# Moving small constants, R's sums and the stores of two output planes in a conditioned residual convolution kernel

## The chip, the cores and the metric

The kernel runs on one core of a Trainium2 chip. The metric is device time in microseconds: the median over several runs, and beside it one execution that was profiled. Engines are named as in the profile: PE is TensorE's matmuls, PEld its weight loads, DVE VectorE, ACT ScalarE, POOL GpSimd, SP SyncE, which issues most DMAs.

## What is computed

128 samples of 64 channels and 1024 positions go through four modulated 1-D convolutions with 3 taps; the input is added to the result. Each sample has its own weights, scaled by a style vector and normalised per output channel.

```python
def _layer(x, style, w, b, mw, mb, typ):
    s = style @ mw.T + mb
    weight = SCALE * w * s[:, None, :, None]
    demod = lax.rsqrt(jnp.sum(weight * weight, axis=(2, 3)) + EPS)
    weight = weight * demod[:, :, None, None]
    if typ == 'same':
        out = jax.vmap(_conv_same)(x, weight) + b[None, :, None]
    elif typ == 'upsample':
        out = jax.vmap(_conv_up)(x, weight.transpose(0, 2, 1, 3)) + b[None, :, None]
        out = _blur(out, 2.0 * blur_k, (1, 1))
    elif typ == 'downsample':
        xb = _blur(x, blur_k, (2, 2))
        out = jax.vmap(_conv_down)(xb, weight) + b[None, :, None]
    return out
...
for i, typ in enumerate(('same', 'upsample', 'same', 'downsample')):
    out = _layer(out, style, weights[i], biases[i], mod_w[i], mod_b[i], typ)
x = x + out
```

## The kernel before

There is no nonlinearity between the layers, so the kernel multiplies the four layers' weights of each sample into one 9-tap filter per pair of channels and convolves once. A few output columns at either end, and the biases, are computed apart. Everything is fp32.

The work goes in 32 groups of 4 samples, numbered q. One pass of the loop (`turn_of`, L1491, here called turn q) works on several groups at once, n = q + 1, c = q + 2 and s = q + 4: it convolves group q to its end and group n in part, and builds the filter of c and, one step further back, of s. The order of instructions on each engine is the order of the code; each engine works its own list through from the top, and waits only for what an instruction needs.

The filter of a group is made in a chain. Stage 1 (`stage1_a`, `stage1_b`, L434 and L448) gives S in the PSUM banks psS; stage 2 (`stage2`, L545) gives R in psR, which ScalarE copies to SBUF (L570). `r_sums` (L615) adds neighbouring slots of R, on GpSimd in a steady turn and on VectorE in turn 4. Stage 3 (`stage3_b`, `stage3_a`, L622 and L647) multiplies R and these sums into the taps Wf, in the banks psA and psW. psS, psR and psW share one pair of PSUM banks, so each has to wait until the last one is read. `combine_a` and `combine_b` (L713, L721) then form three combinations of the taps, h1 to h3, on VectorE; the convolution (`conv0` to `conv4`, L809) works on five combinations of the three input planes with them and with the taps.

An input group lies in one of two buffers X as three planes (every third position). Two of its combinations, T12, are made on GpSimd (`in1`, `in2`), another, T3, in most turns by ScalarE (`in3_negated`, L757) and two accumulating loads that GpSimd issues (`in3_added`, L761); those turns are the set ADDED: 4 to 9, 11 to 13, 16, 17 and 20 to 27. `load` (L141) puts six loads into SyncE's list in each turn, one for each plane and half. `outputs` (L1387) writes one output plane of both halves on ScalarE into a buffer o (two of these) and puts two stores into SyncE's list; planes 2, 1 and 0 follow each other at the end of a turn. So SyncE's list holds six loads and then six stores in each turn.

Turn 4 is the entry, the first pass of this loop (`entry`), and turns 0 to 3 (`early_turn`, L1393) have another order. Beside the turns stand small tables: EXTRA, TABLES, SIDE and LATE (L1316 to L1369) name what is done once, in which turn and where. `small` (L1295) is a small matmul for the constant of one layer into the high columns of the bank Y, `clear_high` (L1304) the memset ahead of it, `small_rest` (L1308) VectorE's use of it. In turns 4, 5 and 6 the matmul stands behind the last conv of the turn, and the rest at the very end of the turn. `tap_differences` (L476) makes differences of blur weights for stage 2, which are first needed in turn 6.

Of the kernel before, what the change touches and what calls it, by code (L numbers as in the profile page):

```python
# [55 lines left out]
K = 3  # L56
# [7 lines left out]
def kernel(  # L64
# [12 lines left out]
    NQ = B // 4  # L77
# [59 lines left out]
    NX = 2  # L137
# [3 lines left out]
    def load(q, planes=slice(0, 3)):  # L141

        if q < NQ:
            at = slice(planes.start * PL, planes.stop * PL)
            for c in range(2):
                nc.sync.dma_start(Xs[q % NX][:, c, at], x[2 * q + c, :, at])
# [117 lines left out]
    def var_newton(bs, ls=slice(0, NL)):  # L264

        newton(var[:, ls, bs], dm[:, ls, bs], nw[:, ls, bs])
# [22 lines left out]
    def table_A(bs, d):  # L289
        table(nc_v, tA, bs, slice(0, 4, 3), slice(1, 3), sc[:, 3, bs], d)  # L290
# [185 lines left out]
    def tap_differences():  # L476

        d = Ed[:, :4].rearrange("c (a b) o -> c a b o", a=2)
        for b in range(2):
            nc_g.tensor_sub(d[:, :, b], E[:, 4 * b : 4 * b + 5 : 4], E[:, 2:7:4])  # L480
        nc_g.tensor_sub(Ed[:, 4:], En[:, 1:4:2], En[:, 2:3].to_broadcast([P, 2, C]))
# [63 lines left out]
    def stage2(q, pool=None, engs=(nc_a, nc_a), between=None):  # L545
        st = chain[q]
        shared = q in shared_ps
        ps = stage2_rest(q) if shared else unit(pool or ps_w, f"psR{q}")
        for n, e in enumerate(() if shared else (-2, -1, 0, 1, 2, 3, 4, 5, 6)):
            if e % 2 == 0:  # L550
                a, lo, m, w = slice(2, 7, 2), e // 2 + 1, 3, E[:, e + 2]
            else:
                a, lo, m = slice(3, 6, 2), (e + 3) // 2, 2
                w = E[:, e + 2] if q in plain else En[:, (e + 1) // 2]
            for r, rows in enumerate(HALF):
                for c, cols in enumerate(HALF):
# [12 lines left out]
        for r in range(2):  # L569
            scaled_copy(engs[r], flat(t[:, r, :7]), ps[r][:, C : 8 * C], tC[:, q, r : r + 1])  # L570
        chain[q] = t
        return ps
# [42 lines left out]
    def r_sums(q, eng):  # L615
        t = chain[q]
        for r in (slice(0, 2),) if eng is nc_v else PAIR:
            eng.tensor_add(t[:, r, 7:10], t[:, r, 0:6:2], t[:, r, 1:7:2])  # L618
# [75 lines left out]
    def residual(q, made):  # L694

        W = Wq[q][0]
        if made:
            v = W[:, tap(1, 1)]
            nc_v.tensor_add(v, v, x3)
            return  # L700
        for r in range(2):
            v = W[:, tap(1, 1), r, :]
            nc_v.scalar_tensor_tensor(v, idn3, t3[:, q, r : r + 1], v, op0=ALU.mult, op1=ALU.add)

    def sum_of(out, x, f, y, op=ALU.add):
        nc_v.scalar_tensor_tensor(out, x, f, y, op0=ALU.mult, op1=op)  # L706
# [3 lines left out]
        merged = (*(W[:, i] for i in TAPS), *(H_[:, i] for i in range(3)))  # L710
        return [t.rearrange("c g r o -> c g (r o)") for t in merged]

    def combine_a(q, made=False):  # L713

        chain.pop(q)
        a, b, c, h1, h2, h3 = taps(q)
        sum_of(h1, c, -2.0, a)
        residual(q, made)
        sum_of(h3, h1, 1.0 / 6.0, b)

    def combine_b(q, steps=range(3)):  # L721
# [140 lines left out]
    def sum2(q, steps=(0, 1), wide=True):  # L862
        if 0 in steps:
            m3 = m3c.pop(q)
            whole = parts(q) if wide else [(s, a[:, :NB]) for s, a in enumerate(banks(q))]
            for s, a in whole:
                sum_of(Y[:, s, :NB], m3[:, s], 3.0, a)
        for s, a in parts(q) if 1 in steps else ():
            nc_v.tensor_sub(y1w[q][:, s], y1w[q][:, s], a)  # L869
# [21 lines left out]
    def store(q, s, planes=slice(0, K), queue=nc.sync):  # L891
        queue.dma_start(
            out[q, :, s, planes.start * NB : planes.stop * NB],
            os[q][:, s, planes].rearrange("c i j -> c (i j)"),
        )
# [41 lines left out]
    def vector_Da(bs):  # L937
        nc_g.tensor_mul(Da[:, bs], sc[:, 3, bs], dm[:, 2, bs])
# [8 lines left out]
    def vector_b1(bs):  # L947
        with_bias(b1s, sc[:, 2], 1, bs)

    def vector_c2(bs):  # L950
        with_bias(c2f, sc[:, 3], 2, bs)
# [352 lines left out]
    def clear_high(q):  # L1304
        _, bs = SMALL[q]
        nc_v.memset(high(bs.stop - bs.start), 0.0)

    def small_rest(q):  # L1308
        l, bs = SMALL[q]
        const_rest(l, bs, high(bs.stop - bs.start))  # L1310

    def layers(i, j):
        return REST, slice(i, j)
# [4 lines left out]
        (1, 1): lambda: (small_rest(1), tap_shares()),  # L1318
        (2, 1): lambda: (small_rest(2), var_root(REST, Y[:, 0])),
        (2, 2): lambda: (table_B(REST), vector_a1(REST)),  # L1320
        (3, 0): lambda: (var_newton(*layers(2, 3)), var_newton(*layers(0, 2))),
        (3, 1): lambda: (table_A(REST, dm[:, 2, REST]), small_rest(3)),
        (3, 2): lambda: (
            table_b(PART[1]),
            (table_0(REST), table_0_kinds()),
            vector_b1(REST),
            vector_c0(REST),
        ),
    }
# [1 line left out]

    TABLES = {
        4: lambda: table_C(REST),
        5: lambda: (vector_c2(REST), vector_Da(REST), table_3(REST), tap_differences()),
        6: zeros,
        7: lambda: table_b(REST),
        9: setup0,
# [4 lines left out]
        4: lambda: var_newton(*layers(3, 4)),  # L1342
    }

    def small_next(q):
        small_rest(q)
        clear_high(q + 1)

    LATE = {
        4: lambda: small_next(4),  # L1350
        5: lambda: small_next(5),
        6: lambda: small_rest(6),
        7: lambda: setup1(0),
        8: lambda: setup_x(0),
        9: lambda: setup_x(1),
# [20 lines left out]

    AHEAD = 3
    FIRST = AHEAD + 1
    ADDED = set(LATE)

    def sharing(q):
        return FIRST < q < NQ - 4
# [4 lines left out]
    def outputs(q, i):  # L1387
        for r in range(2):
            output(q, i, r)
            if late(q):  # L1390
                store(q, r, slice(i, i + 1))

    def early_turn(q):  # L1393
        n, c, s = q + 1, q + 2, q + 3 + (q >= AHEAD)
# [96 lines left out]
    def turn_of(q):  # L1491
        n, c, s = q + 1, q + 2, q + 4
        entry = q == FIRST
        stage2(c)
        if not entry:
            identity(n)
            if q in ADDED:
                in3_negated(c)
            elif s < NQ:
                scale3(s)  # L1500
        if entry:
            sum2(q, wide=False)
            conv4(q)
            combine_a(n)
            r_sums(c, nc_v)
            in3_negated(c)
        else:
            conv2(q)
            r_sums(c, nc_g)
            sum2(q)  # L1510
            in2(n, nc_g)
            if q in ADDED:
                in3_added(c)
        side(TABLES, q)
        if entry:
            in3_added(c)
        for i in range(3):
            load(c + 1, slice(i, i + 1))
        stage3_b(c, open_a(n), c + 1 if sharing(q) else 0)
        if q in ADDED and FIRST < q and s < NQ:  # L1520
            scale3(s)
        if entry:
            conv0(q, 0, 1)
        else:
            combine_a(n, True)
            conv4(q)
        stage3_a(c)
        combine_b(n)
        conv3(n)
        copy_m3(n)  # L1530
        conv0(q, 2 if entry else 0)
        if s < NQ:
            stage1_a(s)
        outputs(q, 2)
        in04(n)
        side(SIDE, q)
        in_g01(c)
        if entry:
            conv1(n, 0, 1)
            outputs(q, 1)  # L1540
        else:
            conv0(q, 1, 2)
        if s < NQ:
            stage1_b(s)
        if entry:
            clear_high(q)
        in_g2(c)
        if sharing(q):
            share_copy(c + 1)
        if not entry:  # L1550
            outputs(q, 1)
        outputs(q, 0)
        if q in SLOTS:
            matmuls, width, rest = SLOTS[q]
            conv1(n, 0, 1)
            slot(matmuls, width, Y_banks)
            rest()
        if s == NQ:
            slot(ends3, 3, unit(ps_w, "psE"), 3)
            rest3()  # L1560
        conv1(n, *((2,) if entry or q in SLOTS else range(K)))
        if q in SMALL:
            small(q)
        sum1(n)
        if q not in ADDED:
            in3(c)
        if sharing(q + 1):
            share_sums(s)
        if s == NQ:
            in04(c)  # L1570
        in1(c, nc_g)
        side(LATE, q)
# [153 lines left out]
```

## Time and profile before

| | |
|---|---|
| median of 3 runs | 477.87 us (477.09 to 479.24) |
| the profiled execution, whole | 477.03 us |
| its span, first to last instruction | 475.3 us |
| PE busy | 465.5 us, 98% |
| DVE, ACT, POOL busy | 399.0, 365.8, 235.0 us |
| granted PE clock, mean | 0.997 |
| moved by DMA | 77.34 MB, mean 163 GB/s |

Durations are read from the profiled execution. A matmul record counts as busy from its start to a modelled end, so a short stop inside a group of matmuls can hide in its busy time; the starts of the groups show it. In a timeline row stand the start in us, the length in us, the engine, the line, the operation, the tiles (output, then inputs) and the count, and in brackets the idle time before it and what ended it. In a row of the waits stand the total in us, how often, and the longest. In a row of a stretch (start:end) stand its length, PE's busy time and matmul records, the granted clock, the mean share of the 16 DMA engines that is busy, and GB/s. [...]

### The profile page before, as it was taken

The numbers are of one execution on the slowest core, as the hardware profiler recorded it, in microseconds if no ns is written. First come the engines' busy times: TensorE is split into PE (matmuls) and PEld (weight loads), VectorE is DVE, ScalarE is ACT, GpSimd is POOL, SyncE is SP. The second block draws the span as 40 slices with busy tenths as digits, with TensorE's granted clock in tenths as the row PEclk, the third lists the DMA queues.
The fourth block names the chain that finished last, engine by engine and source line by source line (L and its number), as shares of the span: only waits on it lengthen the run. The fifth ranks groups of instructions, "written<-read, shape, count | busy, mean of one in ns | idle before, by whom it ended". The sixth has DMA issues, their size and how long they took to land.

```text
span 475.3 us, 26462 instructions
## 1 busy us (share of the span) xinstructions
PE 465.5 (98%) x11656; PEld 346.1 (73%) x11656; DVE 399.0 (84%) x613; ACT 365.8 (77%) x871; POOL 235.0 (49%) x301
## 2 busy tenths in 40 slices
PE   8999999999999999999999999999999999999995
PEld 7977777776677786768867677757677878877652
DVE  4899999878988887888878888969888888988795
ACT  6575667679888896988877988878888889887452
POOL 3534342779755752545444557535455654543200
PEclk9999999999999999999999999999999999999998
DMA  5416264465667654677543675545777567675225
GB/s 176 148 38 224 95 198 188 151 170 141 172 180 203 197 155 147 149 182 201 182 146 126 152 182 182 172 130 123 203 188 186 179 159 196 181 177 160 97 82 192
DMA packets 55986, 77.34 MB, mean 163 GB/s; under 512 B 6272, under 2 KB 52800, under 8 KB 55872
## 3 DMA queue, kind: packets, MB, share of 16 engines
q1 hardware_dynamic: 49808, 68.32, 46.1%
q0 software_dynamic: 5472, 6.66, 9.4%
q8 instruction: 91, 1.49, 1.4%
q10 hardware_dynamic: 592, 0.69, 0.5%
q14 instruction: 23, 0.19, 0.1%
HBM read 42.01 MB, written 33.62 MB: 159 GB/s over the span
## 4 chain that ended last, share of the span: by engine, by line
PE 94%; DVE 3%; issue 1%; DMA 1%; ACT 1%; SPq 0%; ACTq 0%; DVEq 0%
PE psA L809 45%; PE Y L809 11%; PE psW L596 10%; PE psR L490 9%; PE psS L400 5%; PE psR L558 4%; PE psA L596 4%; PE psA L490 2%; PE Y L1052 2%; DMA par_s<-in_params_s 1%; PE Y L337 1%; DVE Y L706 1%; ACT o L887 0%; DVE o L889 0%; DVE H L706 0%
## 5 line engine op out<-in xcount | busy, mean ns | idle before, releaser
L809 PE MATMUL psA<-T,H 64*64 64x340 f32 x2304 | 186.7, 447 | 0.3 <-DVE y L706 0.2
L809 PEld LDWEIGHTS psA<-T,H 64*64 64x64 f32 x2304 | 90.8, 133 | 47.0 <-issue 2.6
L706 DVE SCALAR_TENSOR_TENSOR G<-X 128x684 f32<-128x684 f32 (+1 forms) x65 | 78.4, 1211 | 3.5 <-DMA X<-in_x 0.9
L809 PE MATMUL psA<-T,Wf 64*64 64x340 f32 x768 | 68.1, 446 | 0.0
L809 PE MATMUL Y<-T,Wf 64*64 64x340 f32 x768 | 62.6, 451 | 0.2
L361 ACT ACTIVATE R<-psR,tC 128x448 f32<-128x448 f32 x63 | 36.5, 630 | 31.5 <-PE psR L490 15.1
L465 POOL TENSOR_TENSOR S<-S 128x128 f32<-128x128 f32 x24 | 11.4, 477 | 95.6 <-ACT S L361 95.6
L706 DVE SCALAR_TENSOR_TENSOR Y<-m,psA 128x680 f32<-128x680 f32 (+1 forms) x40 | 29.2, 729 | 28.4 <-PE psA L809 27.4
L796 DVE TENSOR_TENSOR T<-G 128x1368 f32<-128x1368 f32 (+1 forms) x33 | 51.2, 1553 | 0.0
L782 POOL TENSOR_TENSOR T<-G 128x684 f32<-128x684 f32 x28 | 46.4, 1659 | 8.3 <-DVE G L706 8.3
L787 POOL TENSOR_TENSOR T<-G 128x684 f32<-128x684 f32 x28 | 46.6, 1664 | 0.0
L361 ACT ACTIVATE Wf<-psW,t 128x192 f32<-128x192 f32 (+1 forms) x76 | 30.0, 444 | 19.2 <-PE psW L596 18.9
L618 POOL TENSOR_TENSOR R<-R 128x192 f32<-128x192 f32 x48 | 27.8, 599 | 29.2 <-ACT R L361 29.2
L809 PEld LDWEIGHTS Y<-T,Wf 64*64 64x64 f32 x768 | 30.2, 132 | 16.4 <-DVE Y L706 1.1
L887 ACT ACTIVATE o<-psA,tb,td 128x340 f32<-128x340 f32 x63 | 36.1, 622 | 6.3 <-PE psA L809 6.3
L809 PEld LDWEIGHTS psA<-T,Wf 64*64 64x64 f32 x768 | 29.4, 133 | 14.8
L887 ACT ACTIVATE o<-Y,tb,td 128x340 f32<-128x340 f32 x63 | 36.6, 637 | 4.5 <-PE Y L809 2.6
L887 ACT ACTIVATE o<-y,tb,td 128x340 f32<-128x340 f32 x62 | 38.1, 664 | 0.6 <-DVE y L869 0.6
L706 DVE SCALAR_TENSOR_TENSOR H<-Wf 128x384 f32<-128x384 f32 x64 | 38.5, 602 | 0.0
L706 DVE SCALAR_TENSOR_TENSOR H<-H,Wf 128x384 f32<-128x384 f32 x64 | 35.9, 560 | 2.2
L361 ACT ACTIVATE S<-psS,tB 128x256 f32<-128x256 f32 (+1 forms) x63 | 26.8, 476 | 13.0 <-PE psS L400 13.0
L490 PE MATMUL psR<-S,E 64*64 64x64 f32 (+1 forms) x920 | 34.6, 239 | 0.0
(186 smaller groups left out, 1010.6 us busy)
## 6 DMA issues: line engine op xcount, KB each, us to landing
out<-o SPq DMA_DIRECT2D x167, 170.0 KB, 3.0
X<-in_x SPq DMA_DIRECT2D x150, 172.0 KB, 4.5
X<-in_x SPq DMA_DIRECT2D x14, 516.0 KB, 4.5
T<-in_x POOLq DMA_DIRECT2D x38, 171.0 KB, 5.5
out<-o SPq DMA_DIRECT2D x6, 510.0 KB, 5.2
out<-o SPq DMA_DIRECT2D x2, 340.0 KB, 2.7
Xe<-in_x_ends SPq DMA_DIRECT2D x1, 512.0 KB
out<-o ACTq DMA_DIRECT2D x3, 170.0 KB, 2.4
```

The lines of the kernel that those rows point to most:

```text
L361: nc_a.activation(dst, src, AF.Copy, scale=f)
L400: nc.tensor.matmul(ps[r][cols, at * C : (at + n) * C], weight[rows], wd[c if r == 0 else 1 - c][rows, taps], start=first, stop=last, skip_ ...
L490: nc.tensor.matmul(dst[r][cols], weight[rows], st[c if r == 0 else 1 - c][rows, slots, :], start=False, stop=last, skip_group_check=True,)
L558: nc.tensor.matmul(ps[r][cols, (lo + 1) * C : (lo + 1 + m) * C], w[rows], src[rows, a, :], start=(n == 0), stop=(n == 8), skip_group_check ...
L596: nc.tensor.matmul(dst[r][cols], weight[rows], t[rows, c, slots, :], start=first, stop=last, skip_group_check=True,)
L618: eng.tensor_add(t[:, r, 7:10], t[:, r, 0:6:2], t[:, r, 1:7:2])
L706: nc_v.scalar_tensor_tensor(out, x, f, y, op0=ALU.mult, op1=op)
L782: eng.tensor_add(t[:, :, 0, :NJ], plane(g, 2), plane(g, 1))
L787: eng.tensor_sub(t[:, :, 1, :NJ], plane(g, 2), plane(g, 1))
L796: nc_v.tensor_sub(t[:, pairs, :, :NJ], both(a, PL), both(b, 1))
L809: nc.tensor.matmul(ps[s][cols, :NB], w, Ts[q, tag][rows, c, i, g : g + NB], start=(g == 0 and m == 3), stop=(g == K - 1), skip_group_check ...
L887: nc_a.activation(dst, src, AF.Identity, bias=add, scale=d3)
```

## The change

It has five parts.

1. In turn 4 `r_sums` on VectorE goes ahead of the combination h3, by the new argument `ahead` of `combine_a`. In the same turn one group of conv 0 on TensorE moves from ahead of `stage1_a` to behind it, and one group of conv 1 from ahead of `stage1_b` to behind it.
2. `tap_differences` and two constants (`vector_c2`, `vector_b1`) move from turns 5 and 3 (its end) to the middle of turn 3, and `vector_Da` from turn 5 to turn 3.
3. The small matmuls of turns 4, 5 and 6, with what VectorE does with them, move behind stage 2 of the next turn (`small_here`).
4. The stores of planes 1 and 0 in turns 5 to 27 are held back (`to_store`) until the loads of the next turn are in SyncE's list.
5. From turn 5 on GpSimd writes one column of the input buffer behind R's sums (`gate`), a column that the next load writes too. So the loads wait for that write.

```diff
-    def combine_a(q, made=False):
+    def combine_a(q, made=False, ahead=None):
...
         residual(q, made)
+        if ahead:
+            ahead()
         sum_of(h3, h1, 1.0 / 6.0, b)
...
-        (3, 0): lambda: (var_newton(*layers(2, 3)), var_newton(*layers(0, 2))),
-        (3, 1): lambda: (table_A(REST, dm[:, 2, REST]), small_rest(3)),
+        (3, 0): lambda: (
+            (var_newton(*layers(2, 3)), var_newton(*layers(0, 2))),
+            (tap_differences(), vector_c2(REST), vector_b1(REST)),
+        ),
+        (3, 1): lambda: (table_A(REST, dm[:, 2, REST]), small_rest(3), vector_Da(REST)),
...
-        5: lambda: (vector_c2(REST), vector_Da(REST), table_3(REST), tap_differences()),
+        5: lambda: table_3(REST),
...
-    def small_next(q):
+    def small_here(q):
+        small(q)
         small_rest(q)
-        clear_high(q + 1)
+        if q + 1 in SMALL:
+            clear_high(q + 1)
...
             if late(q):
-                store(q, r, slice(i, i + 1))
+                to_store.append((q, r, slice(i, i + 1)))
+        if i == 2 or not FIRST < q < NQ - 4:
+            stores()
+
+    to_store = []
+
+    def stores():
+        while to_store:
+            store(*to_store.pop(0))
+
+    def gate(q):
+        if q < NQ:
+            nc_g.memset(Xs[q % NX][:, :, 0:1], 0.0)
...
         stage2(c)
+        if not entry and q - 1 in SMALL:
+            small_here(q - 1)
...
-            combine_a(n)
-            r_sums(c, nc_v)
+            combine_a(n, ahead=lambda: r_sums(c, nc_v))
...
             r_sums(c, nc_g)
+            gate(c + 1)
             sum2(q)
...
             load(c + 1, slice(i, i + 1))
+        stores()
         stage3_b(c, open_a(n), c + 1 if sharing(q) else 0)
...
-        conv0(q, 2 if entry else 0)
+        if not entry:
+            conv0(q, 0)
...
-            conv1(n, 0, 1)
+            conv0(q, 2)
+            conv1(n, 0)
...
-        conv1(n, *((2,) if entry or q in SLOTS else range(K)))
-        if q in SMALL:
-            small(q)
+        conv1(n, *((1, 2) if entry else (2,) if q in SLOTS else range(K)))
```

How the lists change, at three places. First GpSimd's list in turn 5 and the start of turn 6, before; R is what `r_sums` adds up, T the planes' combinations, c2f and Da the constants, wsq the weight differences, S the sums of stage 1.

```order
L618 TENSOR_TENSOR R_1882<-R_1882 128x192 x2
L787 TENSOR_TENSOR T_6_1839<-G_1798 128x2x342
L765 DMA T_7_1887<-in_x 128x342 x2
L942 TENSOR_TENSOR c2f<-sc,par_s 128x96
L938 TENSOR_TENSOR Da<-sc,dm 128x96
L287 TENSOR_TENSOR t_139<-dm,var 64x48 x2
L284 TENSOR_SCALAR td<-dm 64x48 x2
L480 TENSOR_TENSOR wsq<-E 128x2x64 x2
L481 TENSOR_TENSOR wsq<-En 128x128
L465 TENSOR_TENSOR S_2046<-S_2046 128x2x64
```

The same place after the change:

```order
L618 TENSOR_TENSOR R_1882<-R_1882 128x192 x2
L1406 MEMSET X_107 128x2
L789 TENSOR_TENSOR T_6_1842<-G_1799 128x2x342
L767 DMA T_7_1892<-in_x 128x342 x2
L287 TENSOR_TENSOR t_139<-dm,var 64x48 x2
L284 TENSOR_SCALAR td<-dm 64x48 x2
L465 TENSOR_TENSOR S_2047<-S_2047 128x2x64
```

Four of the operations between R's sums and the next turn's work on S are gone from here, and the write to X stands behind R's sums.

Second SyncE's list from turn 4 on, before; X is an input buffer (two in turn), o an output buffer.

```order
L892 DMA out<-o_1788 128x340 x6
L146 DMA X_107<-in_x 128x344 x6
L892 DMA out<-o_2049 128x340 x6
L146 DMA X_108<-in_x 128x344 x6
L892 DMA out<-o_2340 128x340 x6
```

After:

```order
L894 DMA out<-o_1789 128x340 x6
L146 DMA X_107<-in_x 128x344 x6
L894 DMA out<-o_2050 128x340 x2
L146 DMA X_108<-in_x 128x344 x6
L894 DMA out<-o_2050 128x340 x4
L894 DMA out<-o_2342 128x340 x2
```

The two stores of plane 2 stay at the end of their turn; the four of planes 1 and 0 stand behind the next turn's six loads.

Third VectorE's list in turn 4, before; H are the combinations of the taps Wf, R as above.

```order
L706 SCALAR_TENSOR_TENSOR H_1425<-Wf_1424 128x384
L703 SCALAR_TENSOR_TENSOR Wf_1424<-idn_159,t_139,Wf_1424 128x64 x2
L706 SCALAR_TENSOR_TENSOR H_1425<-H_1425,Wf_1424 128x384
L618 TENSOR_TENSOR R_1652<-R_1652 128x2x192
L706 SCALAR_TENSOR_TENSOR H_1425<-Wf_1424 128x384
```

After:

```order
L706 SCALAR_TENSOR_TENSOR H_1425<-Wf_1424 128x384
L703 SCALAR_TENSOR_TENSOR Wf_1424<-idn_159,t_139,Wf_1424 128x64 x2
L618 TENSOR_TENSOR R_1657<-R_1657 128x2x192
L706 SCALAR_TENSOR_TENSOR H_1425<-H_1425,Wf_1424 128x384
L706 SCALAR_TENSOR_TENSOR H_1425<-Wf_1424 128x384
```

R's sums have gone one step forward.

More of the change, by code (lines that the diff above doesn't have):

```diff
@@ L1325 @@
             (table_0(REST), table_0_kinds()),
-            vector_b1(REST),
             vector_c0(REST),
@@ L1343 @@
     }
-    def small_next(q):
+    def small_here(q):
+        small(q)
         small_rest(q)
-        clear_high(q + 1)
+        if q + 1 in SMALL:
+            clear_high(q + 1)
     LATE = {
-        4: lambda: small_next(4),
-        5: lambda: small_next(5),
-        6: lambda: small_rest(6),
         7: lambda: setup1(0),
@@ L1378 @@
     FIRST = AHEAD + 1
-    ADDED = set(LATE)
+    ADDED = {FIRST, FIRST + 1, FIRST + 2, *LATE}
     def sharing(q):
```

## The prediction

> **What bounds the kernel now.** I read the page first, then TensorE's waits, then the places where TensorE stops, row by row, then the DMA share of single stretches. A turn is one pass of the steady loop; turn 4 is the entry, and turns 8 and 9 serve as examples: the chain of waits has stage 2 of turn 8 at 143.63 and of turn 9 at 157.33, 13.7 us on.
>
> ```profile
> span 475.3 us, 26462 instructions
> PE 465.5 (98%) x11656; PEld 346.1 (73%) x11656; DVE 399.0 (84%) x613; ACT 365.8 (77%) x871; POOL 235.0 (49%) x301
> PE 94%; DVE 3%; issue 1%; DMA 1%; ACT 1%; SPq 0%; ACTq 0%; DVEq 0%
> ```
>
> TensorE is busy for 98% of the span and carries 94% of the chain that ended last. The change removes no matmul, so it can only win back stops. From 88 to 440 us TensorE's waits are three rows:
>
> ```profile
> PE psA L596 <- issue: 1.1, 3, 0.5
> PE Y L1300 <- DVE Y L1306: 0.6, 1, 0.6
> PE psA L596 <- DVE R L618: 0.3, 1, 0.3
> ```
>
> That is 2.0 us of idle time in 352 us. Stops inside a group that counts as busy come on top; I found those by the starts of the same groups in other turns. ```profile
> 143.63 1.94 PE psR L490 x112
> ...
> 157.33 1.94 PE psR L490 x112
> ```
>
> All together the change can win some 3 us, 0.7% of the time. A measurement of this kernel can tell about 0.5% (2.4 us) from no change, so the forecast lies close to that border.
>
> **The entry turn (4).** TensorE's rows there, then VectorE's and ScalarE's:
>
> ```profile
> 91.33 0.58 PE L596 MATMUL psA<-R,w0s 64*64 64x64 f32 x24
> 92.21 0.56 PE L596 MATMUL psA<-R,par 64*64 64x192 f32 x8 [0.29 <-DVE R L618]
> ...
> 96.75 0.80 PE L809 MATMUL psA<-T,Wf 64*64 64x340 f32 x8
> 97.33 0.52 PE L400 MATMUL psS<-wd,par 64*64 64x64 f32 x22
> ...
> 100.61 0.30 PE L1300 MATMUL Y<-c0f,wsum 64*64 64x96 f32 x2 [0.58 <-DVE Y L1306]
> ```
>
> ```profile
> 91.09 0.56 DVE L706 SCALAR_TENSOR_TENSOR H<-H,Wf 128x384 f32<-128x384 f32 x1
> 91.57 0.59 DVE L618 TENSOR_TENSOR R<-R 128x384 f32<-128x384 f32 x1
> ...
> 96.44 0.64 ACT L361 ACTIVATE Wf<-psW,t0c 128x128 f32<-128x128 f32 x2
> ```
>
> - R's sums go ahead of one step of the filter combination, so they start at 91.09 in place of 91.57: 0.48 us earlier. TensorE loses 0.53 us on them (0.88 from 91.33 to 92.21; the same 24 matmuls take 0.35 in turn 8, from 147.10 to 147.45 in the rows further down). Gain 0.48. The step that now comes second feeds the conv of plane 3, whose 24 matmuls end at 96.75; nothing waits for it earlier.
> - The 8 matmuls at 96.75 (0.57 us to 97.33) no longer stand between the conv and stage 1 of the chain. Stage 1 writes the banks that ScalarE reads until 97.08 (96.44 + 0.64), so TensorE, there at 96.75, waits for up to 0.33 us. Both engines move up together, so this stays. Cost between 0 and 0.33; I take 0.3, because the bank of the last read is also needed in the first group.
> - The small matmul no longer waits for the memset at the end of the turn; it is asked for behind the whole of the next stage 2, and the memset is done by then. Gain 0.6. The two later small matmuls move in the same way and cost the same there.
>
> Sum of the entry turn: 0.48 - 0.3 + 0.6 = 0.8 us gained.
>
> **Turn 6.** R's sums are on GpSimd here. TensorE's rows of turn 6, then of turn 8, with GpSimd's sums of turn 6 ahead and its moved work (turn 5, by groups) behind:
>
> ```profile
> 118.75 1.35 POOL L618 TENSOR_TENSOR R<-R 128x192 f32<-128x192 f32 x2
> ```
> ```profile
> 119.60 0.95 PE L596 MATMUL psA<-R,par 64*64 64x192 f32 x5
> ...
> 120.85 1.38 PE L809 MATMUL Y<-T,Wf 64*64 64x340 f32 x16
> ```
> ```profile
> 147.10 0.53 PE L596 MATMUL psA<-R,w0s 64*64 64x64 f32 x24
> 147.45 0.41 PE L490 MATMUL psA<-S,E 64*64 64x64 f32 x16
> ...
> 147.80 0.51 PE L596 MATMUL psA<-R,par 64*64 64x192 f32 x8
> ...
> 148.35 1.95 PE L809 MATMUL Y<-T,Wf 64*64 64x340 f32 x24
> ```
> ```profile
> L480 POOL TENSOR_TENSOR wsq<-E 128x128 f32<-128x128 f32 x2 | 1.5, 774 | 0.1
> L938 POOL TENSOR_TENSOR Da<-sc,dm 128x96 f32<-128x96 f32 x1 | 1.3, 1337 | 0.0
> ```
>
> From the first matmul on the sums to the next conv turn 6 takes 1.25 us (119.60 to 120.85) and turn 8 0.55 (147.80 to 148.35): 0.7 us lost, because GpSimd ends the sums at 120.10. The constants and weight differences of turn 5 (1.5 + 1.3 = 2.8 us, and two shorter operations) had pushed GpSimd back. Moved to turn 3 they fall into this idle time:
>
> ```profile
> 85.79 0.73 POOL L462 TENSOR_TENSOR S<-S 128x256 f32<-128x256 f32 x1 [10.92 <-ACT S L361]
> ```
> ```profile
> POOL S L465 <- ACT S L361: 95.6, 23, 6.4
> ```
>
> Even at twice 2.8 us it fits into 10.9, so turn 3 pays nothing; without that cover it would hold back the chain's sums. What is late next in turn 6 is ScalarE's R, as in turn 8. Gain 0.7.
>
> **The stops called issue.** In turn 9 TensorE stops inside 24 matmuls that depend on nothing new, and again in turn 19, where the group counts as busy:
>
> ```profile
> 160.80 0.51 PE L596 MATMUL psA<-R,w0s 64*64 64x64 f32 x20
> 161.65 0.27 PE L596 MATMUL psA<-R,w0s 64*64 64x64 f32 x2 [0.33 <-issue]
> ...
> 303.76 0.83 PE L596 MATMUL psA<-R,w0s 64*64 64x64 f32 x21
> ```
> ```profile
> 161.40:218.50 57.10, 56.80 (x1528) 1.00 0.61 166
> 218.50:304.05 85.55, 85.34 (x2292) 1.00 0.58 164
> 304.05:362.10 58.05, 57.70 (x1529) 1.00 0.62 166
> ```
> ```profile
> q8 instruction: 42, 0.69, 1.6%
> ```
>
> The stretches run from one such stop to the next (x is TensorE's matmuls). 1528, 2292 and 1529 are 11.9, 17.9 and 11.9 times 128. The instruction queue delivers 42 packets of 16 KB in the same 200.7 us, in which TensorE does 5349 matmuls: 127 to a packet. So the stops stand at packet borders: the next instructions have not arrived. Turn 9's costs 0.5 us (161.65 - 160.80 less 0.35 for the group), turn 19's 0.3 (0.83 against 0.53). The three idle stops sum to 1.1, with 0.33 of idle time for 0.5 lost: 1.1 x 0.5 / 0.33 = 1.7, and 0.3 for turn 19, together 2.0.
>
> [...]
>
> **Why the late stores matter for them.** DMA share of stretches, last but one number (TensorE only): the first two are the start of turn 8 and of turn 9, then two later stretches of turn 8:
>
> ```profile
> 143.90:146.40 2.50, 2.50 (x117) 1.00 0.25 76
> 157.60:160.10 2.50, 2.50 (x117) 1.00 0.64 217
> ...
> 151.60:155.20 3.60, 3.60 (x80) 1.00 0.87 188
> 155.20:157.40 2.20, 2.20 (x56) 1.00 0.38 137
> ```
>
> Turn 9 stops and turn 8 doesn't. At the start of turn 9 the DMA engines are 64% busy with the stores of planes 1 and 0, against 25%. SyncE's rows of turn 8:
>
> ```profile
> 143.81 3.09 SPq L892 DMA_DIRECT2D out<-o  x4
> 146.99 4.06 SPq L146 DMA_DIRECT2D X<-in_x  x6
> ```
>
> After the change the four stores stand behind the six loads, and the loads wait for GpSimd's write of a column behind R's sums. In turn 8 those sums lie ahead of the matmuls on them at 147.80, so the loads, which before start at 146.99, start up to 0.8 us later. The start of the turn, where stage 2 and stage 3 use up instructions fastest (117 matmuls in 2.5 us against 80 in 3.6), is then free of stores and loads. I count the 2.0 us as won, less 0.1 for a remainder: 1.9.
>
> Everything behind the gate has cover. GpSimd waits 95.6 us for stage 1 in 23 turns, 4.2 a turn; the memset that its next step waits behind fits in (no 128x2 memset is in the trace; it costs between 0 and the 0.7 of one of R's two sums, and either fits). The loads are read first in the next turn, and a turn is 13.7 us against the 4.06 that they take to issue. The stores free an output buffer that is written again two turns on.
>
> **What it costs.** The four stores do not vanish. Two plane 2 stores are what the stretch 155.2 to 157.4 holds: 0.38 x 2.2 = 0.84 us of all engines, so four take 1.7. They now follow loads and GpSimd's accumulating loads, where the share is 0.87, and fill the quieter 155.2 to 157.4 (1.36 us free). The instruction packet asked for in the second half of a turn, which now finds that quiet stretch, has to pass them. Only turns with accumulating loads are that full: 18 of them (5 to 9, 11 to 13, 16, 17, 20 to 27). Bounds: no stop, or 0.5 us (turn 9's) in all 18, 9.0. I take two to three stops, 1.2 us, the end that is nearer to turn 8, which goes through a stretch of 0.87 without a stop.
>
> Sum: 0.8 + 0.7 + 1.9 - 1.2 = 2.2 us gained. The profiled execution took 477.03 (1.7 beside its span), 0.8 below the median of 477.87; it would take 474.8. Taken off the median: **475.7**.
>
> **Rivals.**
> - The late stores cost no packet: gain 3.4, 474.5, and 473.4 if a second stop in turn 19 and delays under 0.3 us, which I left out, go too. For it: turn 8 runs through its full second half without a stop. [...]
> - The late stores stop TensorE at the turn's end instead: the packet comes behind six loads and four stores. It decides from 7 turns with a stop (3.4 / 0.5); 12 to 18 of them give 6 to 9 less 3.4, so 480.5 to 483.5. For it: 1.7 us of stores meet 1.36 us of free engines before the next turn.
> - The stops are not due to data traffic, so that part of the change does nothing: 0.8 + 0.7 gained, 476.4. Against it: the multiples of 128.
>
> **How the numbers follow.** Forecast 0.48 (gain 1.0 to 3.0; 0.12 of it beyond 2.4), no cost 0.24, stops at the turn's end 0.20, no link to traffic 0.08. Faster by over 0.5%: 0.12 + 0.24 = 0.36. Slower: 0.20. Within 0.5%: 0.36 + 0.08 = 0.44. The range runs from the free case with its small delays, 473.4, to 15 turns with a stop (7.5 - 3.4 = 4.1), 482.0; about 0.1 is left out above and 0.08 below.
>
> **What would show it.** Right: the waits lose the rows for the memset and VectorE's R, turn 6 takes 13.7 us, no stop called issue near the start of turns 9, 13, 19 and 23, and DMA share under 0.3 there. Wrong: stops at packet borders during the last conv of a turn or in stage 2 (the rival), or the same stops as before. A time under 473.4 or over 482.0 would mean that I mis-sized the stops or the traffic.

## The result and the profile after

| | before | changed |
|---|---|---|
| median of 6 runs each | 477.48 us (476.30 to 479.24) | 483.12 us (481.65 to 485.21) |
| span of the profiled execution | 475.3 us | 481.3 us |

The changed kernel is slower: the ratio to before is 1.0118, with an interval of 1.0085 to 1.0151. That is 5.6 us more, where 2.2 us less were forecast, and 1.1 us beyond the upper end of the range.

The page of the changed kernel, its span, its busy times and its chain by engine:

```profile
span 481.3 us, 26509 instructions
PE 467.4 (97%) x11656; PEld 355.3 (74%) x11656; DVE 398.8 (83%) x613; ACT 365.6 (76%) x871; POOL 235.2 (49%) x325
PE 93%; issue 2%; DVE 2%; DMA 1%; ACT 1%; ACTq 0%; DVEq 0%
```

No engine has more work: VectorE, ScalarE and GpSimd are busy for as long as before to within 0.2 us, and TensorE does the same 11656 matmuls. What grew is the word "issue" in the chain. TensorE's waits from 88 to 440 us name the place:

```profile
PE psR L490 <- issue: 4.7, 7, 1.0
PE psA L596 <- issue: 0.8, 4, 0.3
PE psA L490 <- issue: 0.6, 2, 0.3
```

The rows for the memset and for VectorE's R are gone, as forecast. But 6.1 us of issue stand where 1.1 stood, and 4.7 of them in stage 2 (psR, L490), a group that had no such row before.

**The gains came.** Chain of waits, stage 2 of turns 6 and 7, before and then after:

```profile
115.26 0.08 PE psR L490
...
129.90 0.07 PE psR L490
```
```profile
114.75 1.94 PE psR L490 x112
128.54 1.93 PE psR L490 x100
```

Turn 6 went from 14.6 to 13.8 us. For the entry, TensorE's rows of stage 2 of turns 4 and 5, before and after, and one row of turn 3 after:

```profile
87.12 2.73 PE L558 MATMUL psR<-S,E 64*64 64x192 f32 x72
...
100.64 0.38 PE L558 MATMUL psR<-S,E 64*64 64x192 f32 x2
```
```profile
85.85 0.80 PE L811 MATMUL psA<-T,H 64*64 64x340 f32 x8 [0.16 <-DVE y L706]
...
87.82 2.71 PE L558 MATMUL psR<-S,E 64*64 64x192 f32 x72
...
100.21 0.59 PE L558 MATMUL psR<-S,E 64*64 64x192 f32 x8
```

Turn 4 takes 12.4 us in place of 13.5.

**Where the time went.** The stops now follow each other at one distance. Four neighbouring stretches of the changed kernel, each from one stop in stage 2 to the next (x is the matmuls):

```profile
374.70:389.50 14.80, 14.24 (x382) 1.00 0.64 172
389.50:404.20 14.70, 14.21 (x382) 1.00 0.65 171
404.20:418.90 14.70, 14.03 (x382) 1.00 0.65 174
418.90:433.70 14.80, 14.04 (x382) 1.00 0.65 170
```

382 is 2.98 times 128, a multiple as the stretches of the kernel before were: TensorE stops at every third packet border. A turn here is about three packets long, so from turn 24 to 28 the same border falls into stage 2 turn after turn, and the turn takes 14.7 us in place of 13.7. From turn 5 to 28 the trace has 14 gaps of over 0.33 us between two matmul starts at packet borders, together 9.4 us: 7 of them in stage 2 (6.3 us) and 7 in the first groups of stage 3 (3.1 us), where the kernel before stopped too.

The same turn, 24, cut into five stretches at about the same points of the work, before and after (the last but one number is the DMA share; it adds up the times of the packets that start in a stretch, and so can exceed 1). Stage 2 starts at 372.26 before; after, it starts at 373.83 and has just stopped at a border from 374.46 on, so that the cut begins inside this stop:

```profile
372.40:374.40 2.00, 2.00 (x120) 1.00 0.58 196
374.40:376.40 2.00, 2.00 (x53) 1.00 0.51 178
376.40:380.40 4.00, 4.00 (x110) 1.00 0.85 221
380.40:383.40 3.00, 3.00 (x72) 1.00 0.96 202
383.40:386.40 3.00, 3.00 (x73) 1.00 0.38 126
```
```profile
374.70:376.70 2.00, 1.77 (x94) 1.00 0.18 63
376.70:378.70 2.00, 2.00 (x59) 1.00 0.00 0
378.70:382.70 4.00, 4.00 (x104) 1.00 0.57 119
382.70:385.70 3.00, 3.00 (x72) 1.00 0.98 218
385.70:388.70 3.00, 3.00 (x70) 1.00 1.08 364
```

The first 4 us are empty now, and the last 3 us, which were quiet, are full. The last two stretches as one line each, 40 slices of 0.15 us, a digit for the tenths of busy DMA engines; before, then after:

```profile
DMA  6969979999999998865641500000000008998997
```
```profile
DMA  9899899889986888899999999999999999999999
```

Before there is a hole of ten slices, 1.5 us, between the loads of the turn and the two stores of plane 2 that end it. In the changed kernel there is none. The row of the instruction queue, in a window of 0.1 us each, tells when the packet of this part of the turn starts: before at 383.7 to 383.8, in the falling share just ahead of the hole, after at 387.3 to 387.4, with all engines busy.

```profile
q8 instruction: 1, 0.02, 59.9%
```
```profile
q8 instruction: 1, 0.02, 61.2%
```

The border lies 28 matmuls into the next stage 2. TensorE's rows around it, before (where nothing stops) and after:

```profile
386.00 0.51 PE L490 MATMUL psR<-S,E 64*64 64x128 f32 x16
...
386.45 0.40 PE L490 MATMUL psR<-S,E 64*64 64x128 f32 x8
```
```profile
388.89 0.28 PE L490 MATMUL psR<-S,E 64*64 64x128 f32 x2
389.93 0.33 PE L490 MATMUL psR<-S,E 64*64 64x128 f32 x2 [0.76 <-issue]
```

After, 389.93 - 387.35 = 2.6 us pass from the packet's start to the first matmul out of it. Before, the 29th matmul of stage 2 comes at about 386.5, 2.75 us behind the packet's start, and TensorE doesn't stop. In the changed kernel TensorE is at the border at 388.95, 1.6 us behind the packet's start. The packet starts 1.2 us nearer to its border than before, and TensorE waits 1.0 us for it.

### The profile page after: what moved, and what is told of

Read it like the earlier page. It is cut to its first block, busy times and chain, and to the rows that moved or that the text cites. A ratio compares the mean times of both kernels' runs of the same rounds, so it can differ in the third digit from the quotient of the medians.

```text
span 481.3 us, 26509 instructions
## 1 busy us (share of the span) xinstructions
PE 467.4 (97%) x11656; PEld 355.3 (74%) x11656; DVE 398.8 (83%) x613; ACT 365.6 (76%) x871; POOL 235.2 (49%) x325
## 4 chain that ended last, share of the span: by engine, by line
PE 93%; issue 2%; DVE 2%; DMA 1%; ACT 1%; ACTq 0%; DVEq 0%
PE psA L811 44%; PE Y L811 12%; PE psR L490 10%; PE psW L596 10%; PE psS L400 5%; PE psR L558 5%; PE psA L596 4%; PE psA L490 2%; PE Y L1054 2%; DMA out<-o 1%; ACT o L889 1%; PE Y L337 1%; PE Y L180 1%; PE psM L204 0%; DVE o L891 0%
## 5 line engine op out<-in xcount | busy, mean ns | idle before, releaser
L811 PEld LDWEIGHTS psA<-T,H 64*64 64x64 f32 x2304 | 95.8, 133 | 43.4 <-issue 2.0
L465 POOL TENSOR_TENSOR S<-S 128x128 f32<-128x128 f32 x24 | 11.8, 490 | 96.4 <-ACT S L361 96.4
L490 PE MATMUL psR<-S,E 64*64 64x64 f32 (+1 forms) x920 | 36.4, 240 | 1.4 <-issue 1.4
L361 ACT ACTIVATE S<-psS,tB 128x256 f32<-128x256 f32 (+1 forms) x63 | 26.8, 476 | 13.5 <-PE psS L400 13.4
```

Source lines behind the costliest of these rows:

```text
L361: nc_a.activation(dst, src, AF.Copy, scale=f)
L490: nc.tensor.matmul(dst[r][cols], weight[rows], st[c if r == 0 else 1 - c][rows, slots, :], start=False, stop=last, skip_group_check=True,)
L811: nc.tensor.matmul(ps[s][cols, :NB], w, Ts[q, tag][rows, c, i, g : g + NB], start=(g == 0 and m == 3), stop=(g == K - 1), skip_group_check ...
```

## The experiments

The theory after this: three kinds of traffic (loads behind the gate, accumulating loads, late stores) are pressed together until the next plane 2 stores and close the hole, so that the instruction packet, which started as the share fell, starts late. The rivals: the late stores alone do it, the gate alone does it, or the stops have nothing to do with the traffic. All edits are against the changed kernel. Ratios are to the kernel before on the same chip, with their intervals; "issue" is the sum of TensorE's waits of that name from 88 to 440 us in the profiled execution, and one execution can lie off the median: 488.39 us for the merged stores with the late gate, 484.39 for the border shift.

| kernel | median, us | ratio | issue, us |
|---|---|---|---|
| the change | 483.12 | 1.0118 [1.0085, 1.0151] | 6.1 |
| moves only | 475.14 | 0.9968 [0.9951, 0.9986] | 0.7 |
| late stores, no gate | 476.14 | 0.9995 [0.9976, 1.0014] | 0 |
| gate only | 476.78 | 0.9996 [0.9979, 1.0013] | 2.7 |
| four stores left out | 473.12 | 0.9920 [0.9904, 0.9936] | 0 |
| no accumulating loads | 473.49 | 0.9914 [0.9891, 0.9937] | 0 |
| early gate | 474.77 | 0.9960 [0.9942, 0.9978] | 0 |
| gate between the sums | 483.48 | 1.0111 [1.0075, 1.0147] | 6.0 |
| later gate | 484.57 | 1.0122 [1.0083, 1.0160] | 6.2 |
| one late store | 477.89 | 1.0011 [0.9984, 1.0037] | 2.4 |
| two late stores | 483.97 | 1.0134 [1.0102, 1.0166] | 8.4 |
| merged stores, late gate | 484.10 | 1.0138 [1.0091, 1.0185] | 10.4 |
| merged stores, no gate | 474.58 | 0.9948 [0.9928, 0.9967] | 0.3 |
| merged stores, early gate | 475.00 | 0.9955 [0.9932, 0.9978] | 0.3 |
| border shift | 487.35 | 1.0214 [1.0179, 1.0249] | 4.0 |
| border shift, early gate | 476.73 | 0.9990 [0.9970, 1.0010] | 0.2 |

**The parts taken apart.** Moves only:

```diff
-        if i == 2 or not FIRST < q < NQ - 4:
-            stores()
+        stores()
...
-            gate(c + 1)
```

> Only parts 1 to 3 of the change (entry order, constants, small matmuls); stores and loads as before, no write ahead of the loads. If the late stores and the gate cost the time: 1.5 us less than before (0.8 in turn 4, 0.7 in turn 6), so a ratio near 0.997 and the four stops called issue near the start of turns 9, 13, 19 and 23 still there. If the moves cost the time: 4 to 6 us more than before.

Parts 1 to 3 gain 0.32%, 1.5 us, which is the 0.8 and 0.7 of the forecast. Three waits called issue are left, where I had expected four. Parts 4 and 5 together therefore cost 1.5% of 477.5, 7.2 us. Each of them alone, first the late stores (only `gate(c + 1)` is taken out), then the gate (only the two lines with `stores()` are undone):

> The whole change without the write ahead of the loads: the loads then start with the turn and the four stores follow them. If the late place of the stores delays instruction packets at the turn's end: the second half is less full since loads start 4 us earlier, so stops in stage 2 go, but loads now stand at the start of the turn, where turn 9 stopped before; time between before and after, about 479. If the gate alone costs the time: as before less 1.5, about 476. If the stores cost it wherever the loads are: 483, as after.

> Parts 1 to 3 and the gate, stores at their old place. Loads start at 4.1 us of each turn in place of 0.4 to 4.1. If the late stores cost the time: within 1 us of the moves alone (476), since the second half holds the same loads as before, at most 2 us later in a turn. If it is the later loads: 481 or more.

The late stores without the gate took 476.14 us, the time that I had given for the rival that the gate alone costs the time; the gate alone, at 476.78, refutes it, though it lies 1.6 us above the moves alone and not within 1. Over the moves alone the late stores cost 0.27% and the gate 0.28%, 1.3 us each and hardly more than the intervals. Together they would make 2.6 us, and they make 7.2: the larger part belongs to neither part, but to the two together. The late stores by themselves left no stop at all called issue in the profile (0 us from 88 to 440). That the loads then start early in the turn, and the stores behind them are through in time, is my reading of the lists; no row of this run shows it. The same two stretches of turn 24 with the gate only; the hole is there, with a tenth of the engines busy in it:

```profile
DMA  9979997549999999999999978311111002998899
```

**One kind of traffic taken away.** The stores of planes 1 and 0 in turns 5 to 27 left out, and, in another kernel, the accumulating loads left out:

```diff
-            if late(q):
+            if late(q) and (i == 2 or not FIRST < q < NQ - 4):
```
```diff
-            if q in ADDED:
-                in3_added(c)
         side(TABLES, q)
```

> The whole change, but the stores of planes 1 and 0 of turns 5 to 27 are left out, so that those output planes are not written. 7.8 MB of 33.6 written go away. If stores behind the loads delay the instruction packets: the stops in stage 2 vanish and so do those at the start of the turn, about 474 (before less 3.4). If the stops come from the loads and accumulating loads behind the gate, stores or no stores: 481 to 483, as after.

> The whole change without the accumulating loads of turns 5 and later (GpSimd's two DMA issues a turn that add tap 3's share are left out, so that part of the output isn't computed); gate, loads and late stores as in the changed kernel. Crowding: the third party of the crowd is gone, the loads and late stores are through by about +11 us, the packet asked for at about +9 arrives in time; idle time called issue on psR in stage 2 falls from 4.7 us to under 1, time 474 to 477. Order (loads behind the gate with stores behind them are enough by themselves, the accumulating loads have no part): stops stay, over 3 us of issue, 480 to 483.

Both kernels have no wait called issue from 88 to 440 us, and they are 0.8 and 0.9% faster than before. (The first writes 17.6 MB in place of 33.6, so 16.0 are left out, twice what I had written.) In the second one the gate, the loads and the four late stores stand as in the change; so their order alone does not stop TensorE. Its two stretches of turn 24:

```profile
DMA  9899799934986899998998998744444307996998
```

The share falls to four tenths for a microsecond, the packet starts just ahead of this, at 380.5, and nothing stops. (When a packet is asked for stands in no trace; the +9 was my estimate.) So the full cost needs all three kinds.

**The time of the gate.** The gate ahead of R's sums, between the two of them, and one step later:

```diff
-            r_sums(c, nc_g)
             gate(c + 1)
+            r_sums(c, nc_g)
```
```diff
         for r in (slice(0, 2),) if eng is nc_v else PAIR:
+            if r == PAIR[1]:
+                gate(q + 1)
...
-            gate(c + 1)
```
```diff
-            gate(c + 1)
             sum2(q)
             in2(n, nc_g)
+            gate(c + 1)
```

> The whole change, but the write stands ahead of R's sums on GpSimd, so that the loads start about 2 us into the turn in place of 4.1; the late stores then also run 2 us earlier. If the transfers are pressed against the turn's end: half or more of the loss goes, 477 to 480. If the late place of the stores costs the time whatever the time of the loads: 483. If the gate matters only by holding the loads at all: 483.

> The whole change with the gate between the two sums of R on GpSimd, one sum of about 0.7 us earlier than in the changed kernel and 1.35 us later than in the kernel with the early gate; the loads then start at about +3.4 us of a turn, near the +3.3 to +3.8 of the kernel before. Crowding by degrees (each bit of room at the end of the turn counts): between the two, 476 to 480, with 1 to 3 us called issue. A step between +3.4 and +4.1: as fast as the early gate, 474 to 476. A step between +2.0 and +3.4: as slow as the whole change, 481 to 485.

> The whole change with the gate one step later on GpSimd (behind the sums and the product that follow R's sums), so that the loads start about 1 to 2 us later than +4.1 us of a turn, and the late stores behind them. Crowding by time: 2 us earlier gave 474.77, 0 gave 483.12, so later is worse, 484 to 490, with more than 4.7 us of issue on psR in stage 2, stores' data past +13.5. Saturated (once the packet is late, later traffic costs no more; half of the late stores cost as much as all of them): 482 to 484. Falling again (the packet of the second half passes ahead of the loads): under 480.

In the trace the loads start at 2.0, 3.5, 4.1 and 5.7 us of a turn (early gate, between the sums, the change, later gate), and the ratios are 0.9960, 1.0111, 1.0118 and 1.0122. Almost all of the cost arises between 2.0 and 3.5 us, and from there on it hardly grows. The loads of the kernel before start at 3.5 us too in many turns (146.99 - 143.63 = 3.4 in turn 8), but there the stores are out ahead of them. "Crowding by degrees" fails. The early gate came out below all three ranges that I had given, with the whole loss gone; the median of the later gate lies in the range of "crowding by time", but its ratio is that of the change, so the cost is saturated. SyncE's rows of turn 24 show what the gate does to its list, first the change, then the early gate:

```profile
378.70 4.29 SPq L146 DMA_DIRECT2D X<-in_x  x6
383.09 4.63 SPq L894 DMA_DIRECT2D out<-o  x6
```
```profile
372.70 1.39 SPq L146 DMA_DIRECT2D X<-in_x  x3
374.19 8.20 SPq L894 DMA_DIRECT2D out<-o  x6
```

In the change the loads go out from 378.70 to 383.0 and the six stores one behind the other up to 387.7: the four late ones run into the two of plane 2. The last two stretches of the turn with the early gate, and with the gate between the sums:

```profile
DMA  9899999998899999999543250000000007998997
```
```profile
DMA  9999899999679999999999999999998475997799
```

With the early gate the hole is as wide as before the change, and no stop is left. With the gate between the sums it shrinks to three slices of four to seven tenths, and the packet comes too late. The later gate doesn't fit this picture; its last two stretches of turn 24:

```profile
DMA  5799699999998699999999999999999999999999
```

There is no hole, and still the packet starts at 386.7, 11.9 us behind the start of stage 2 (11.8 with the gate only), and TensorE doesn't stop at its border; this kernel stops in other turns (6.2 us of issue). So a mean share of the 16 engines doesn't fix when a packet starts.

**The amount of the late stores.** One and two of the four stay late (`if i or not FIRST < q < NQ - 4` ahead of `stores()`; for one, the first half's store of plane 0 is sent at once too), and all of their bytes in half as many stores:

```diff
-            if late(q):
-                to_store.append((q, r, slice(i, i + 1)))
-        if i == 2 or not FIRST < q < NQ - 4:
+            if late(q) and not (pair and i == 1):
+                to_store.append((q, r, slice(0, 2) if pair and i == 0 else slice(i, i + 1)))
+        if i == 2 or not pair:
             stores()
```

> The whole change, but only plane 0's two stores stand behind the loads; plane 1's stay at the end of their turn. If the crowding of the second half costs the time: between the gate alone (476.8) and after (483), about 479 to 480, with fewer and shorter stops in stage 2. If it is the order of the two kinds on the queue, whatever the amount: 482 to 483.

> The whole change with one store a turn behind the loads (plane 0 of the second half), the three others at their old place. Crowding by bytes: a quarter of the late stores, 478 to 480 between the gate alone (476.78) and the whole change (483.12). Saturated (half of the late stores cost as much as all): 481 to 485. Only the gate matters below some amount: 475.5 to 477.5.

> The whole change, gate as in the changed kernel, with planes 1 and 0 of a half in one store of 680 columns: the same bytes behind the loads, half as many stores and packets twice as long. Crowding by bytes: as slow as the changed kernel, 481 to 485. Crowding by packets or descriptors: half the crowd that the late stores make, 476 to 480, and the last 3 us of a turn well under the full share that they have in the changed kernel.

Again a step: one late store costs 0.43% over the moves alone, little more than the gate does without any, and two cost as much as four. My expectation of half the cost for half the stores was wrong. Half as many stores of twice the size cost as much as the four. That doesn't decide between bytes and count, because two stores of the old size cost as much as well. Turn 24 with one late store, and with two:

```profile
DMA  9953478879999999999999999664442100001998
```
```profile
DMA  9999999939999967978999999999954435999999
```

With one the hole is open; with two it is five slices of three to five tenths, and the packet starts only behind them, at 390.1. The longest stops of all stand in that kernel, TensorE's row in turn 24:

```profile
376.69 0.27 PE L490 MATMUL psR<-S,En 64*64 64x64 f32 x1 [2.13 <-issue]
```

**Other ways to make room.** The merged stores without the gate, and the merged stores with the early gate:

> The moves alone (parts 1 to 3), with planes 1 and 0 of a half written by one store of twice the size behind the last output, in place of two; no gate and nothing behind the loads. If instruction packets and transfers collide at the start of a turn: plane 1's stores no longer run there, so the three stops that the moves alone kept go, 0.5 to 1.5 us less than the moves alone, about 474. If only the amount of transfers counts: as the moves alone, 475.1.

> The whole change, but with the gate ahead of R's sums (loads at +2.0 us of a turn) and with planes 1 and 0 of a half in one store of 680 columns (two late stores a turn in place of four). Crowding (loads, accumulating loads and late stores pressed into one stretch delay the instruction packet): both edits take traffic out of the stretch from +8 to +14 us, so no stop over 0.5 us in turns 5 to 28 and 473.5 to 474.8, as fast as the better of the two alone (474.58 and 474.77) or up to 1 us better. Borders (a packet border in stage 2 costs a stop whatever the traffic, and the two fast kernels were lucky in their phase): the phase is that of the early gate with fewer stores, stops of some sum between 1 and 6 us return, 475.5 to 480.

Both have the hole, and both are about half a per cent faster than before; so is the early gate with four stores. The three intervals and that of the moves alone overlap, so none of the three is shown to beat the moves alone, and two edits against the same crowd gain no more than one. The expectation "up to 1 us better" for the pair did not come true.

**The place of the borders.** 32 small matmuls of zeros in the setup (64 matmul records more, 11720 for 11656) move every packet border by half a packet, in the change and in the kernel with the early gate:

```diff
     zeros_to_y(2, 128, False)
+    zeros_to_y(16, 4, False)
```

> The whole change with 32 small matmuls of zeros more in the setup, where TensorE waits anyway: 128 instructions on TensorE, so half an instruction packet. If the stops stand at packet borders: none is left at the matmuls where after stops (stage 2's and stage 3's first groups), all stand 64 matmul records from there, still multiples of 128 apart, and the time may change by several us either way. If the stops belong to those instructions (a buffer, a bank, a result that they wait for): same places, same time as after.

> The kernel with the early gate (474.77) and the 32 small matmuls of zeros in the setup that move every packet border by half a packet; with the late gate they took the time from 483.12 to 487.35. Crowding: without a crowd the place of the borders is of little account, 474.5 to 476.5, idle time called issue under 1.5 us from 88 to 440. Borders (the early gate was lucky in its phase): several us of stops return at the borders' new places, 477.5 to 482.

Stretches between stops in the shifted change:

```profile
203.80:218.50 14.70, 14.20 (x382) 1.00 0.67 171
...
350.40:365.30 14.90, 14.39 (x382) 1.00 0.64 169
```

The stops are again three packets apart, but fall on other matmuls than in the change: counted from the first instruction of the program, the added ones included, they stand at the same fraction of a packet. All ten of the waits called issue are in stage 2 (psR), at other matmuls of it; that none would be left in stage 2's groups did not come true. So they belong to the borders and not to what the matmuls at that place wait for. The shift costs 0.96% (4.6 us) with the late gate and 0.30% (1.4 us) with the early one. In the traces the added matmuls themselves take 2.4 and 2.3 us, since TensorE did not wait in the setup as I had assumed: stage 2 of turn 4 starts at 90.22 in place of 87.82, and at 90.17 in place of 87.91. So with the late gate some 2.2 us are left for the place of the borders, no more than the two intervals allow for noise (0.48%, 2.3 us), and with the early gate nothing. The profiled execution of the shifted change has less issue than the change, 4.0 us against 6.1. So where the stops fall follows the borders; that the place of the borders costs time is not shown.

## Why the prediction was wrong

- **Entry turn, 0.8.** Right in the sum, with more on each side: turn 4 gained 1.1 us and turn 3 lost 0.3 to 0.4: it went from 87.12 - 72.16 = 15.0 to 87.82 - 72.50 = 15.3 us by the starts of stage 2 of turn 3 in the chains of waits below, before and after; the row at 85.85 waits for VectorE's y there. That "turn 3 pays nothing" was not quite so.

```profile
72.16 2.50 PE psR L558 x72
```
```profile
72.50 2.50 PE psR L558 x72
```

- **Turn 6, 0.7.** Right: 14.6 to 13.8 us. The moves alone gained 1.5 us, as the two terms say.
- **The stops called issue are packet borders.** Right, and borne out by the border shift, and by the trace of the change, where each of the 14 stops ends 1.2 to 1.6 us after the end of an instruction packet. The rival without a link to traffic falls: issue went from 0 to 10.4 us among kernels that compute the same with the same matmuls (11656 records before and after the change), by where and when their traffic lies.
- **1.9 us won at the start of the turn.** In turn 24 the share fell (0.58 to 0.18, counted from inside its first stop), but 7 stops of the old kind, in the first groups of stage 3, are still there. The start of a turn was not emptied: the stores of plane 2, which end a turn, are pressed back by the late ones and run over into the next. Turn 23 of the changed kernel:

```profile
359.80:361.60 1.80, 1.80 (x105) 1.00 0.79 250
361.60:363.60 2.00, 2.00 (x58) 1.00 0.03 8
```

The packet starts at 361.6, as these stores end, and TensorE stops at its border from 363.6 to 364.0. Filling the end of a turn undid the clearing of the next start.

- **What it costs, 1.2 us: the step that failed.** "I take two to three stops, 1.2 us, the end that is nearer to turn 8, which goes through a stretch of 0.87 without a stop." Measured for parts 4 and 5 together: 7.2 us lost, net, where these two terms (1.9 - 1.2) gave 0.7 gained. As a cost that is inside the bounds of 0 and 9.0 that I had given, at the far end, and the price of a stop was too low as well: the 14 stops took 9.4 us, 0.67 each, where I had put 0.5. The sum behind it had an item missing. I moved the four stores, 1.7 us of all engines, into 1.36 us of free share. But the gate moves the loads as well, and I had counted their later start without their traffic. In turn 24 the first 8 us carry 2 x 0.18 + 4 x 0.57 = 2.6 us of traffic in place of 2 x 0.58 + 2 x 0.51 + 4 x 0.85 = 5.6: 3.0 us had to find room later. The stretch from 8 to 11 us was at 0.96 already, and the last 3 us had 3 x 0.62 = 1.9 free. So it overflowed. And turn 8 was no witness: its packet starts at 155.0, as the share falls behind the full stretch, and the change fills the place where it fell.
- **The rival on the other side** (480.5 to 483.5, from 7 turns with a stop on) is the number that was measured, and half of its mechanism: 14 stops over 0.33 us, 483.12, but only 7 of them in stage 2, behind the crowded end of a turn. I gave it 0.20, though its own sentence, 1.7 us of stores against 1.36 free, spoke for it.
- **The rival that the late stores cost no packet** rested on turn 8, which goes through its full second half without a stop; beyond that it was my estimate. The runs speak against it: with the late stores behind gated loads the packet starts 1.2 us nearer to its border in turn 24, and two late stores or more cost 1.2 to 1.4% where the gate alone costs nothing against before.
- **The cover behind the gate** held: the memset takes 0.1 us on GpSimd, and TensorE has no wait on GpSimd. What I did not follow up is SyncE's own wait, one row of its list:

```profile
SPq L146 <- POOL X L1406: 108.7, 24, 6.6
```

4.5 us a turn in which SyncE could have sent stores: in turn 24 ScalarE has written the last of the four by 375.8, while the loads, which stand ahead of them in the list, go out from 378.7 and the stores from 383.1.

What stays open: the packet starts as the share falls, or just ahead of that, in the five profiles of turn 24 with a hole, and late in the three where it is closed or shrunk; but with the later gate it starts in time without a hole. So that traffic delays the packets is shown by the edits, and what in the traffic lets one packet through is not. Nor is it settled whether bytes or number of stores count, and why the late stores without a gate, with no stop left, still run 0.27% behind the moves alone; the two intervals overlap.

## What to carry to other kernels

Before traffic is moved, add up all that moves with it, and look for the last quiet place ahead of the next burst: the instruction queue may be living from it, as here the packet at 383.7 in turn 24, just ahead of a hole of 1.5 us. TensorE, 98% busy before the change and 97% after, was still stopped by its own instructions, for 9.4 us in 14 stops; the sign of it was an idle row called issue at distances near multiples of 128 matmuls (1528, 2292, 382). When two edits each press on the same quiet place, test them together as well as alone, since neither showed here what both did: 1.3 us each, 7.2 together.

## What the runs showed of the hardware that was not expected

- The cost of late packets did not grow evenly: loads at 3.5 rather than 2.0 us of a turn cost 1.5%, two late stores rather than one 1.2%, and more of either added next to nothing.
- In the trace of the changed kernel TensorE goes on 1.2 to 1.6 us after the end of the packet that it waits for, in each of the 14 stops; the packet itself takes 1.0 to 1.3 us. From the start of the packet to TensorE's next matmul these stops show 2.3 to 2.8 us.
- 32 matmuls of no use in the setup cost the changed kernel 1%, half of it by their own 2.4 us; what the place of the borders adds lies within the noise.
- GpSimd's memset of 128x2, whose price I had bounded by 0 and 0.7 us, takes 0.1 us.
